# Layer 1's first half: one list of tokens for the experts, or one for each quarter

## The chip, the cores and the metric

The kernel runs on one core of a Trainium2 chip. It is one launch that computes a whole network of four layers. The metric is the device time of that launch in microseconds, as the median of several runs. A core has a matrix engine (TensorE, PE in the profile, with its weight loads as PEld), three engines for elementwise work (VectorE as DVE, ScalarE as ACT, GpSimd as POOL) and SyncE (SP), which here only issues transfers. Every engine runs its own instructions in order and waits on semaphores for the others.

## The reference

Input and output are x of shape (4, 1024, 128) in float32. Each of the four layers does two steps, and after each step x becomes layernorm(x + step(x)):

- Layer 0: a scan over the sequence with a small positional basis ("l0_attn"), then a linear layer whose input and weight are rounded to six-bit values with one scale for 32 of them ("l0_ffn").
- Layer 1: a diagonal complex state-space scan ("l1_attn"), then a mixture of experts.
- Layer 2: causal attention with 16 heads and rotary positions ("l2_attn"), then a mixture of 8 experts with low-rank corrections, 2 per token.
- Layer 3: a Toeplitz mix, then a mixture of 32 experts, 4 per token.

The change is about layer 1's mixture. It has 16 experts of width 128 in four groups. A token takes the two best groups, and in them its four best experts:

```python
scores = sigmoid(x @ router_w.T)          # (tokens, 16)
# two groups by the sum of their two best (scores + bias), then 4 experts
tw = scores[chosen] / sum(scores[chosen]) * 2.5
routed = sum_e tw[e] * (silu(x @ gate_w[e]) * (x @ up_w[e])) @ down_w[e]
out = routed + (silu(x @ sh_gate) * (x @ sh_up)) @ sh_down
```

No step of layer 1 or of layer 0 mixes tokens backwards in time: a token depends on earlier positions of its own row only.

## The kernel before

x stays in on-chip memory as 32 tiles of 128 tokens by 128 values. The sequence is cut into four quarters of 256 positions; with the 4 rows of the batch a quarter is 8 tiles. The same first half (quarters 0 and 1, `self.first`, a `Part` named "a") goes through layer 0 and layer 1's scan, and then its experts run while the second half (quarters 2 and 3) is still in layers 0 and 1.

Layer 1's experts work on a list in device memory. For a part with nt tiles:

- `l1_route` (from L751) computes scores, groups, the mask of the four experts and the weights on DVE; `positions` (L1235) turns the mask into a position in the list for each token and expert (L1276), so that tokens of one expert lie together and every expert begins at a multiple of 128 rows. It also writes the expert of each list tile (`ids`) and the number of list tiles in use (`used`).
- `spread` (L1313) copies token rows to their places: four indirect transfers per tile, issued on POOL (L1301).
- `small_experts` (L1718) walks over the list in groups of four list tiles. `inputs` loads a group (L1332, on SP; the load waits for all the scatters of the list) and transposes it on PE; `up` does the gate and up products on PE, silu on ACT (L1748) and the product with it on DVE (`hg`, L1749); `turn` transposes the result; `down` does the last product, copies it out of PSUM (L1763 on ACT or L1766 on DVE, `yg`) and stores it on SP (L1767). Two groups are loaded ahead.
- A list has room for every possible routing, (nt x 128 x 4 + 127 x 16) rows rounded up to 4 tiles. `small_experts` runs straight-line over the likely length, nt x 4 + 8 tiles rounded up to 4; for what may lie above that, `rest_of` (L1354) puts one `If` on all engines, each of which reads `used` first (L1358, the branch shows as L1359). It then marks the list as made.
- `collect` (L1381) brings results back: four gathers per tile on POOL (L1301, into one buffer `yt` of the pool `yp`, of which there are five) and four adds per tile on DVE (L1392), x += weight x row. The gathers wait for the stores of the list. `l1_close` (L829) collects a quarter at a time, normalizes it (L192 to L209), stores it (`xsave`, L836) and transposes it for layer 2.

The order on each engine is the order in which Python generators are run. `mix` (L238) runs a main generator and, after each of its steps, as many steps of a side generator as the step's estimated microseconds times a pace pay for; instructions of the side are ordered behind those of the main that were already issued. `chain` runs generators one after the other, `abreast` runs several side by side by their estimated times, and `when` (L1819) yields idle steps until a condition holds. The work around the change is, in `all` (L1887 to L1914):

1. `l1_route(a)` after l1_attn of quarters 0 and 1.
2. l0_attn of quarters 2 and 3, with the scatters of list a beside it.
3. The shared experts and the experts of list a as main; beside them l0_ffn and then l1_attn of quarters 2 and 3, at pace 2.0 and without draining what is left.
4. What is left of that side, abreast with `l2_weights` (L1418), as main, with `l1_close(a)` beside it. `l2_weights` builds 24 blocks of layer 2's expert weights: a scaled copy on ACT (L1434), products on PE into a PSUM tile "s", a copy to `we` on ACT (L1444; three buffers), a store on SP (L1446). PSUM has two buffers of the tag "s", which l0_ffn, l1_attn, `turned` and `l2_weights` share in this stage.
5. Layer 2's attention for the first half of the heads' work, `l2_attn(0)` (its first rotation is L928). It begins with normalized quarters 0 and 1.

l0_ffn's rounding (`quantize`) is a chain between DVE and POOL: L483 to L486 on DVE, L489 on POOL, L492 to L496 on DVE, L499 on POOL, L500 on DVE, L501 on POOL, L502 and L503 on DVE. After it POOL adds the bias (L529). l1_attn of a quarter begins with PE products that DVE takes up at L645, scans at L649, turns at L660 to L668, adds at L676 and norms at L209.

Of the kernel before, what the change touches and what calls it, by code (L numbers as in the profile page):

```python
# [40 lines left out]
E1, F1, NG1, TKG1, K1 = 16, 128, 4, 2, 4  # L41
# [15 lines left out]
class Part:  # L57
# [3 lines left out]
    def __init__(self, name, q0, nq, rows=None, lg0=None):  # L61
        self.name, self.q0, self.nq, self.lg0 = name, q0, nq, lg0
        if rows is None:
            self.order = list(range(q0 * QT, (q0 + nq) * QT))
        else:
            self.order = [tile_of(b, 2 * q + k) for b in rows for q in range(q0, q0 + nq) for k in range(2)]
        self.t0, self.nt = q0 * QT, len(self.order)
# [7 lines left out]
class Kernel:  # L75
    def __init__(self, ctx, tc, ins, out, cols, consts, rows):
        self.tc, self.nc, self.ins, self.out = tc, tc.nc, ins, out
        self.count = itertools.count()
        nc = self.nc
        self.const = self.pool(ctx, "const")  # L80
        self.small = self.pool(ctx, "small", 3)
        self.routes = self.pool(ctx, "routes")
        self.side = self.pool(ctx, "side", 2, space=PSUM)
        dram = self.pool(ctx, "dram", space=DRAM)

        self.cols_t = self.load(self.const, ins["cols"])
        self.cst_t = self.load(self.const, ins["consts"])
        self.x = self.tile(self.const, [P, NT, D], "x")
        self.xT = self.tile(self.const, [P, NT * P], "xT")
        nrow = ins["rows"].shape[1]  # L90
        self.rows_t = self.tile(self.const, [P, nrow], "rows")
        nc.gpsimd.dma_start(out=self.rows_t, in_=ins["rows"].to_broadcast([P, nrow]))
        self.col = {k: self.cols_t[:, a:b] for k, (a, b) in cols.items()}
        self.cst = {k: self.cst_t[:, a:b] for k, (a, b) in consts.items()}
        self.row = {k: self.rows_t[:, a:b] for k, (a, b) in rows.items()}
        self.ident = self.cst["ident"]
        self.eps = self.tile(self.const, [P, 1], "eps")
        nc.vector.memset(self.eps, LN_EPS)
        self.halfpi = self.tile(self.const, [P, 1], "halfpi")
        nc.vector.memset(self.halfpi, math.pi / 2)  # L100
        self.ones = self.tile(self.const, [P, E3], "ones")
        nc.vector.memset(self.ones, 1.0)
        self.rnd = self.tile(self.const, [P, 1], "rnd")
        nc.vector.memset(self.rnd, RND)
        self.zero = self.tile(self.const, [P, D], "zero")
        nc.gpsimd.memset(self.zero, 0.0)
        self.flag = self.tile(self.const, [1, 1], "flag", I32)
        self.hm = self.tile(self.const, [P, 4], "hmg")

        self.first, self.rest = Part("a", 0, 2), (Part("b", 2, 1), Part("c", 3, 1))  # L110
        self.parts = (self.first, *self.rest)
        self.by_rows = (
            Part("a", 0, 2, range(B), 0), Part("m", 2, 2, (0, 1), NT // 2), Part("n", 2, 2, (2, 3), 3 * NT // 4)
        )

        self.rows_done = 0

        self.listed = set()

        self.traced, self.latest = nc.cur_bb.bb.instructions, {}  # L120
        self.now = self.moved_by = 0.0
        self.moved = []

        self.lists, self.route = {}, {}
        self.both = (self.first, Part("r", 2, 2))
        for lay, ne, k in (("l1", E1, K1), ("l2", E2, K2), ("l3", E3, K3)):
            for pt in {"l1": self.both, "l2": self.by_rows, "l3": self.parts}[lay]:
                tl = -(-((pt.nt * P * k + (P - 1) * ne) // P) // 4) * 4
                self.lists[lay, pt.name] = (
                    self.tile(dram, [tl * P, D], f"{lay}r{pt.name}"), self.tile(dram, [tl * P, D], f"{lay}y{pt.name}"), tl  # L130
                )
        self.wall2 = self.tile(dram, [P, E2 * 3 * F2], "wall2")
        self.xsave = self.tile(dram, [P, NT, D], "xsave")

        self.ksave = self.tile(dram, [P, B, BLK], "ksave")
        self.vsave = self.tile(dram, [P, B, 4, (NH + 1) * VW], "vsave")
# [1230 lines left out]
    def zero_lists(self, *lays):  # L1367

        for (lay, name), (rows, ys, tl) in self.lists.items():
            if lay not in lays:  # L1370
                continue
            part = next(p for p in (*self.parts, *self.by_rows, *self.both) if p.name == name)
            ne, k = {"l1": (E1, K1), "l2": (E2, K2), "l3": (E3, K3)}[lay]
            for t, at in ((rows, 0), (ys, self.likely(part, ne, k))):
                if at < tl:
                    self.nc.sync.dma_start(
                        out=t[at * P :, :].rearrange("(t p) d -> p t d", p=P),
                        in_=self.zero.unsqueeze(1).to_broadcast([P, tl - at, D]),
                    )
# [507 lines left out]
    def all(self):  # L1887
        a, rest = self.first, self.rest
        b, c = rest
        r = self.both[1]  # L1890
        a2, m2, n2 = self.by_rows
        with ExitStack() as ctx:
            lgp = self.pool(ctx, "l2lg")
            self.l2_lg = self.tile(lgp, [P, NT, E2], "lg")
            with ExitStack() as early:

                self.l0_setup(early)
                self.l2_wr = self.load(lgp, self.ins["l2_wr"])
                self.run(self.l0_attn((0, 1)))
                self.l1_setup()  # L1900
                self.l2_setup()
                self.zero_lists("l1")
                self.run(self.l0_ffn((0, 1)))
                self.run(self.l1_attn((0, 1)))

                self.run(self.l1_route(a))
                self.run(self.mix(self.l0_attn((2, 3)), self.spread("l1", a, K1)))
                self.zero_lists("l2", "l3")
                with ExitStack() as c2:
                    wall = self.l1_wall(c2)  # L1910
                    yp = self.pool(c2, "l1ya", 5, right=True)
                    side = self.chain(self.l0_ffn((2, 3), True), self.l1_attn((2, 3), True))
                    self.run(self.mix(self.chain(self.l1_shared(a), self.l1_experts(a, wall)), side, 2.0, False))
                    self.run(self.mix(self.abreast(self.l2_weights(), side), self.l1_close(a, yp)))  # L1914
            with ExitStack() as c2:
                wall = self.l1_wall(c2)
                self.run(self.mix(self.l2_attn(0), self.chain(self.l1_route(r), self.spread("l1", r, K1))))
                wall2, loads = self.l2_wall(c2, True)
                yp = self.pool(c2, "l1yr", 5, right=True)
                self.run(self.mix(self.chain(self.l1_experts(r, wall), self.l1_shared(r)), self.chain(loads, self.routed(a2))))  # L1920
                self.run(self.mix(self.l2_experts(a2, wall2), self.l1_close(r, yp)))
            listed = lambda name: lambda: name in self.listed
# [6 lines left out]
            with ExitStack() as c3:  # L1929
                with ExitStack() as c2:  # L1930
                    wall = self.l2_wall(c2)
# [7 lines left out]
                yp = self.pool(c3, "l3y", 8)  # L1939
# [25 lines left out]
        with self.tc.If(bad > 0):  # L1965
            with ExitStack() as ctx:
# [9 lines left out]
                for p in self.parts:  # L1976
                    self.run(self.onward(p))
                    with ExitStack() as c2:
                        sw, wall = self.l3_wall(c2)
# [167 lines left out]
```

## Time and profile before

The runs before took 2413.85, 2411.06 and 2410.7 us, a median of 2411.06. The profiled execution took 2413.21 us; its span, from the first to the last instruction on record, is 2411.4 us.

| engine | busy us | share of the span |
|---|---|---|
| PE | 1616.9 | 67% |
| DVE | 1263.6 | 52% |
| ACT | 825.0 | 34% |
| POOL | 722.6 | 30% |

The mean granted TensorE clock is 0.818 of full speed. The stages around the change, by the timeline of the trace:

| stage | from | to |
|---|---|---|
| l1_route(a) on DVE | 245.57 | 275.3 |
| scatters of list a (64) | 268.9 | 381.2 |
| first load of the list; first up-product | 411.93 | 424.87 |
| experts, 18 groups, to the last store | 424.87 | 501.9 |
| gathers (64) | 505.25 | 622.94 |
| last add of the list | 624.65 | 625.0 |
| L928, first rotation of l2_attn(0) | 632.63 | |

How to read the rows that are shown below: a timeline row has start, duration, engine, line, operation, output and inputs by the program's names, and in brackets the engine's idle time before it and what ended it. "issue" and "remote" are idle times that the profile can put down to nothing it records. A row of waits says which engine and line waited for which, how long in total, how many times and the longest. A row of a tile has the shortest, median and longest duration in ns.

### The profile page before, as it was taken

Reading aid. Unit: us, or ns where it says so; the run is one execution under the profiler, and the core shown is the slowest. Engines: PE = TensorE matmul, PEld = TensorE weight load, DVE = VectorE, ACT = ScalarE, POOL = GpSimd, SP = SyncE. Lnnn points to the kernel's source line nnn. Section 1 sums busy time; section 2 is a strip of 40 time slices with the busy share of each in tenths; the row PEclk is TensorE's granted clock in tenths of the full one; section 3 lists DMA queues with packets and bytes.
Section 4 is the critical chain, followed back from the end, with each engine's and each line's share of the span. In section 5 each row is a group of like instructions: output and inputs, shape, how many; then the busy total and the mean of one; then the engine's idle time right before and its main releaser. Section 6 shows DMA issues by size and latency. Waiting matters only on the chain. (4 is left out here: it accounts for less than half of the span.)

```text
span 2411.4 us, 27036 instructions
## 1 busy us (share of the span) xinstructions
PE 1616.9 (67%) x9017; PEld 967.3 (40%) x9017; DVE 1263.6 (52%) x3630; ACT 825.0 (34%) x1180; POOL 722.6 (30%) x681
## 2 busy tenths in 40 slices
PE   7626876975661778487969787887745798357160
PEld 3214333853320337345623232344523486245160
DVE  8957894655570565224545675473611265236233
ACT  6701571422330333122236564642201164223030
POOL 1031484135227000435132002002272200735725
PEclk9856887988785888788979998988977899678575
DMA  9930002334101016212130000031321131222232
GB/s 309 288 112 0 20 34 90 112 115 160 62 31 53 15 34 200 83 44 74 38 106 21 1 1 16 3 114 40 143 85 35 44 112 46 76 79 62 89 89 68
DMA packets 215530, 187.10 MB, mean 78 GB/s; under 512 B 16528, under 2 KB 194064, under 8 KB 214864
## 3 DMA queue, kind: packets, MB, share of 16 engines
q1 hardware_dynamic: 194672, 142.29, 18.7%
q0 software_dynamic: 20704, 42.86, 5.8%
q8 instruction: 84, 1.38, 0.2%
q14 instruction: 70, 0.57, 0.1%
HBM read 88.49 MB, written 96.60 MB: 77 GB/s over the span
## 5 line engine op out<-in xcount | busy, mean ns | idle before, releaser
L1055 ACT ACTIVATE pr<-sc 128x1024 f32<-128x1024 f32 x288 | 279.7, 1021 | 319.9 <-PE sc L157 184.9
L157 PE MATMUL gu<-ld,xgT 128*128 x640 | 177.4, 423 | 88.8 <-issue 38.7
L157 PE MATMUL sc<-qm,kT 32*128 32x512 f32 (+3 forms) x1536 | 199.2, 558 | 13.7 <-issue 12.3
L157 PE MATMUL s<-pr,va 128*32 128x512 f32 (+3 forms) x1536 | 177.1, 528 | 46.0 <-issue 26.2
L157 PEld LDWEIGHTS gu<-ld,xgT 128*128 128x128 f32 x640 | 127.5, 210 | 119.1 <-issue 49.7
L165 PE MATMUL tp<-ld,hg 128*128 128x128 f32 x624 | 104.0, 289 | 92.1 <-ACT hT L167 38.0
L169 DVE COPY hT<-tp 128x512 f32<-128x512 f32 x118 | 81.0, 686 | 159.3 <-remote 73.9
L157 PE MATMUL gu<-wall,xgT 128*128 x304 | 156.1, 640 | 2.7 <-ACT xgT L167 2.0
L1061 DVE TENSOR_TENSOR pr<-pr,ld 128x512 f32<-128x512 f32 (+1 forms) x160 | 92.2, 581 | 100.6 <-ACT pr L1055 98.5
L165 PEld LDWEIGHTS tp<-ld,hg 128*128 128x128 f32 x624 | 81.5, 149 | 144.7 <-issue 46.9
L165 PE MATMUL tp<-ld,xg 128*128 128x128 f32 x396 | 68.9, 305 | 102.1 <-DMA xg<-l3rc 48.5
L1749 DVE TENSOR_TENSOR hg<-sg,gu 128x256 f32<-128x256 f32 x160 | 65.8, 417 | 134.9 <-ACT sg L1748 95.8
L167 ACT COPY xgT<-tp 128x512 f32<-128x512 f32 x99 | 58.0, 586 | 213.0 <-PE tp L165 91.1
L157 PEld LDWEIGHTS sc<-qm,kT 32*128 32x128 f32 x1536 | 84.8, 197 | 113.6 <-issue 77.4
L1507 ACT ACTIVATE sg<-gu 128x512 f32<-128x512 f32 x76 | 45.2, 597 | 225.7 <-PE gu L157 109.4
L1748 ACT ACTIVATE sg<-gu 128x256 f32<-128x256 f32 x160 | 61.1, 385 | 163.2 <-PE gu L157 80.9
L1301 POOL DMA_INDIRECT l1ra<-x,posl1a x64 | 93.1, 1455 | 59.5 <-DVE posl1a L1276 40.3
L157 PEld LDWEIGHTS s<-pr,va 128*32 128x32 f32 x1536 | 38.9, 113 | 156.6 <-issue 109.5
L1509 DVE TENSOR_TENSOR hg<-sg,gu 128x512 f32<-128x512 f32 x76 | 51.7, 682 | 92.1 <-ACT sg L1507 48.7
L1301 POOL DMA_INDIRECT yt<-l1yr,posl1r x64 | 60.9, 951 | 124.1 <-DVE x L1392 79.3
L165 PEld LDWEIGHTS tp<-ld,xg 128*128 128x128 f32 x396 | 52.4, 158 | 107.6 <-issue 59.0
L1301 POOL DMA_INDIRECT l1rr<-x,posl1r x64 | 61.7, 965 | 99.5 <-DVE posl1r L1276 80.3
(440 smaller groups left out, 3498.8 us busy)
## 6 DMA issues: line engine op xcount, KB each, us to landing
wall<-wall SPq DMA_DIRECT2D x16, 768.0 KB
l3ra<-zero SPq DMA_DIRECT2D x1, 6144.0 KB
ld<-in_l_w SPq DMA_DIRECT2D x2, 3072.0 KB
wall<-we SPq DMA_DIRECT2D x24, 256.0 KB
ld<-in_l_w SPq DMA_DIRECT2D x1, 6144.0 KB
l1ra<-zero SPq DMA_DIRECT2D x1, 5120.0 KB
l1rr<-zero SPq DMA_DIRECT2D x1, 5120.0 KB
xg<-l3ra SPq DMA_DIRECT2D x20, 256.0 KB
```

Source lines behind the costliest of these rows:

```text
L157: return self.nc.tensor.matmul(out, lhsT, rhs, start=start, stop=stop)
L165: nc.tensor.transpose(pt[:, k * P : (k + 1) * P], s, self.ident)
L167: nc.scalar.copy(dst, pt[:, : n * P])
L169: nc.vector.tensor_copy(dst, pt[:, : n * P])
L1055: nc.scalar.activation(pr, sc[h], AF.Exp)
L1061: nc.vector.tensor_tensor(d, d, cst["tril"].unsqueeze(1).unsqueeze(1).to_broadcast([P, 2, n, P]), ALU.mult)
L1301: ins = self.nc.gpsimd.indirect_dma_start(**kw)
L1507: nc.scalar.activation(sg, gu[:, 0, :], AF.Silu)
L1509: nc.vector.tensor_tensor(h, sg, gu[:, 1, :], ALU.mult)
L1748: nc.scalar.activation(sg, pg[:, :, 0, :], AF.Silu)
L1749: nc.vector.tensor_tensor(h[:, 2 * c : 2 * c + 2, :], sg, pg[:, :, 1, :], ALU.mult)
```

## The change

The first half gets two lists, "a0" for quarter 0 and "a1" for quarter 1, in place of list "a"; the second half's list "r" stays. Both are routed one after the other at the place where "a" was routed, and their scatters follow each other beside l0_attn. The experts of a0 and then those of a1 run as the main work. The side of that stage gets a second strand beside l0_ffn and l1_attn: when list a0 is made, `l1_close(a0)` begins, with the same five buffers. What is left of both strands goes on in the next stage, whose own side is now only `l1_close(a1)`. By the formulas above a list of 8 tiles has 48 tiles of room and a likely length of 40, ten groups; a list of 16 tiles has 80 and 72, 18 groups.

```diff
+        self.early = (Part("a0", 0, 1), Part("a1", 1, 1))
...
-            for pt in {"l1": self.both, "l2": self.by_rows, "l3": self.parts}[lay]:
+            for pt in {"l1": (*self.early, self.both[1]), "l2": self.by_rows, "l3": self.parts}[lay]:
...
-            part = next(p for p in (*self.parts, *self.by_rows, *self.both) if p.name == name)
+            part = next(p for p in (*self.parts, *self.by_rows, *self.both, *self.early) if p.name == name)
...
-                self.run(self.l1_route(a))
-                self.run(self.mix(self.l0_attn((2, 3)), self.spread("l1", a, K1)))
+                self.run(self.l1_route(a0))
+                self.run(self.l1_route(a1))
+                self.run(self.mix(self.l0_attn((2, 3)), self.chain(self.spread("l1", a0, K1), self.spread("l1", a1, K1))))
                 self.zero_lists("l2", "l3")
                 with ExitStack() as c2:
                     wall = self.l1_wall(c2)
                     yp = self.pool(c2, "l1ya", 5, right=True)
-                    side = self.chain(self.l0_ffn((2, 3), True), self.l1_attn((2, 3), True))
-                    self.run(self.mix(self.chain(self.l1_shared(a), self.l1_experts(a, wall)), side, 2.0, False))
-                    self.run(self.mix(self.abreast(self.l2_weights(), side), self.l1_close(a, yp)))
+                    listed = lambda name: lambda: name in self.listed
+                    side = self.abreast(
+                        self.chain(self.l0_ffn((2, 3), True), self.l1_attn((2, 3), True)),
+                        self.chain(self.when(listed("made l1a0")), self.l1_close(a0, yp)),
+                    )
+                    both = self.chain(self.l1_shared(a), self.l1_experts(a0, wall), self.l1_experts(a1, wall))
+                    self.run(self.mix(both, side, 2.0, False))
+                    self.run(self.mix(self.abreast(self.l2_weights(), side), self.l1_close(a1, yp)))
```

More of the change, by code (lines that the diff above doesn't have):

```diff
@@ L1890, in all @@
         r = self.both[1]
+        a0, a1 = self.early
         a2, m2, n2 = self.by_rows
```

## The prediction

> **What bounds the kernel now.** I read the windows table first, split where the work around layer 1's experts changes hands: experts alone (440 to 470), experts with a quantise chain beside them (470 to 505), then the collecting of the list beside the layer 2 weights and layer 1's attention of quarters 2 and 3 (505 to 625). Columns: stretch, length, busy time and count of PE, weight loads, VectorE (DVE), ScalarE and GpSimd (POOL), TensorE clock, DMA share, GB/s.
>
> ```profile
> 440.00:470.00 30.00, 29.54 (x202) 27.30 (x201) 21.28 (x70) 14.37 (x31) 1.19 (x1) 1.00 0.48 143
> 470.00:505.00 35.00, 26.63 (x181) 23.20 (x180) 26.23 (x61) 10.86 (x23) 8.30 (x4) 0.99 0.31 92
> 505.00:540.00 35.00, 23.38 (x76) 12.42 (x77) 14.88 (x36) 7.84 (x19) 22.39 (x20) 0.77 0.38 130
> 540.00:580.00 40.00, 34.12 (x136) 18.88 (x135) 27.77 (x90) 12.00 (x28) 23.44 (x21) 0.96 0.53 180
> 580.00:625.00 45.00, 11.85 (x41) 6.09 (x39) 20.68 (x96) 7.46 (x13) 23.86 (x24) 0.65 0.35 112
> ```
>
> The experts are bound by PE (29.54 of 30 us). Behind them nothing is full: PE 69.35, DVE 63.33, POOL 69.69 of 120 us. That stage is set by order, so I read what waits in it: the waits from 497 to 640 (total, times, longest), then the gathers on POOL and DVE's timeline.
>
> ```profile
> ACT we L1444 <- issue: 47.7, 11, 12.5
> PE s L165 <- DVE x L209: 36.7, 3, 19.7
> POOL yt L1301 <- DVE x L1392: 29.4, 2, 17.0
> POOL yt L1301 <- DMA l1ya<-yg: 22.0, 1, 22.0
> ```
>
> ```profile
> 505.25 1.01 POOL L1301 DMA_INDIRECT yt<-l1ya,posl1a  x1 [21.98 <-DMA l1ya<-yg]
> 506.56 0.96 POOL L1301 DMA_INDIRECT yt<-l1ya,posl1a  x1 [0.30 <-issue]
> ...
> 550.47 0.95 POOL L1301 DMA_INDIRECT yt<-l1ya,posl1a  x1 [17.03 <-DVE x L1392]
> ...
> 606.26 0.95 POOL L1301 DMA_INDIRECT yt<-l1ya,posl1a  x1 [12.37 <-DVE x L1392]
> ```
>
> ```profile
> 518.69 1.29 DVE L645 TENSOR_TENSOR b<-s,wi 128x512 f32<-128x512 f32 x2 [11.05 <-PE s L157]
> ...
> 548.27 2.19 DVE L1392 SCALAR_TENSOR_TENSOR x<-yt,wkl1a,x 128x128 f32<-128x128 f32 x8
> ```
>
> The 64 gathers start 3.4 us after the last expert work (501.9) and come 1.25 us apart, 80 us in all; they stop twice, because the adds that free the five buffers stand in DVE's order behind quarter 2's attention (548.27) and quarter 3's (602). So two things in series set the stage: layer 1's attention, quarters 2 then 3, and the last gathers. Layer 2's attention takes its first rotation (L928) at 632.63, which is 127.4 us after the first gather. From there both kernels have the same order on every engine, so a shift of L928 should reach the end unchanged.
>
> One stretch is unlike the rest:
>
> ```profile
> 590.08 0.17 DVE L177 TENSOR_SCALAR rstd<-rstd 128x8 int32<-128x8 int32 x1 [1.85 <-remote]
> 590.28 0.43 DVE L908 MEMSET va<- 128x448 f32 x1
> 592.90 0.24 DVE L180 TENSOR_TENSOR nwt<-rstd 128x8 f32<-128x8 f32 x1 [2.18 <-issue]
> ```
>
> From 580 to 598 DVE gets one small instruction per 2 us and PE waits 19.7 us for L209; ScalarE's copies of the weights unit (L1444) have three of their 11 gaps here, up to 12.5 us. It follows the 3 MB load issued at 569.15. In 543 to 546 the same chain runs at 0.2 us an instruction, so this costs about 18 us. The trace does not show what starves it.
>
> **Routing (two lists).** List 1 is quarter 0's, list 2 quarter 1's. A list for each quarter runs the routing code twice. Quarter 0's part can fill DVE's idle 4.28 us before 232.9 and 5.49 us before 245.57. Routing before takes DVE from 245.57 to 275.3, some 30 us, about a third in pieces whose cost hardly shrinks with half the tokens (60 instructions at 0.15 to 0.3 us, 0.7 to 0.8 of their time again: 7 to 9 us), and two more activation-table loads at 1.28 us stand on ScalarE. The z-projections of l0_attn queue on PE behind quarter 0's mask products. l0_attn beside the scatters is DVE-bound (37.71 of 40 us in 300 to 340), so what DVE loses is passed on. Bounds 0 and 9 us; I take **+4**, since the idle stretches hide about half. The scatters start earlier and are not on the path: experts wait for the shared experts' weights, and the first expert load is held by PE until 411.93.
>
> **Two more groups and a middle If.** With 16 tiles the list's likely length is 72 tiles, 18 groups of four; with 8 it is 40, so 10 + 10. SP's expert stores give the pace (and where the quantise chain slows it):
>
> ```profile
> 466.52 0.36 SPq L1767 DMA_DIRECT2D l1ya<-yg  x1
> 468.44 0.36 SPq L1332 DMA_DIRECT2D xg<-l1ra  x1
> 469.95 0.36 SPq L1767 DMA_DIRECT2D l1ya<-yg  x1
> 471.98 0.36 SPq L1332 DMA_DIRECT2D xg<-l1ra  x1
> 478.37 0.36 SPq L1767 DMA_DIRECT2D l1ya<-yg  x1
> ```
>
> A group costs 3.54 us, so two cost 7.1. Its tenth store goes out at 469.95: call that E'. After it every engine meets an If; SP cannot issue list 2's first loads before it, where now they are three groups ahead. Refill: store to next transfer 1.7 us (as at 501.9 to 503.59), load 3.3 (a store of the same 256 KB: from 501.9 to the gather it lets go at 505.25), transposes and copy 3 (L165 x8 takes 1.91 us), so the first up-product is at E'+8; from there to the first store 10.5 us (424.87 to 435.34), then 9 periods: E'+50.4 = 520.4, against 501.9. That is **+18.5**, if nothing holds list 2's experts.
>
> What the branch itself costs: DVE passed the If with 0.19 us (row below) and SP with at most 1.7.
>
> ```profile
> 504.21 0.17 DVE L182 TENSOR_SCALAR nwt<-nwt 128x8 f32<-128x8 f32 x1 [0.19 <-DVEq L1359]
> ```
>
> The Trainium skill ("Runtime: NRT & Kernel Launch", Instruction fetch mechanics) speaks against this part: a taken branch whose target lies outside the two prefetched pages stalls the engine for a fetch from memory. By that rule a further stall of a transfer's length, some 2 us by the 1.7 us row, would fall on the PE or DVE and the total be +2. The If here skips the same two groups as the one measured, so I keep the row: nothing beyond the refill.
>
> **Collecting list 1 beside list 2.** In the built order POOL has, between the two Ifs, 16 gathers (tiles 0 to 3) mixed with the quantise steps L499 and L501, and after the second If four more that need no store of list 2. So 20 of quarter 0's 32 gathers may run beside experts; 12 stay, with quarter 1's 32: 44 gathers or 55 us remain, instead of 80. But DVE's order puts 4 adds of tile 0, L500 (which waits for POOL's L499, behind two gathers of tile 1) and 3 adds of tile 1 ahead of list 2's first hg product, and the rest of the adds between the next ones. The gathers begin at E'+3.4; with 1.25 us each, 2.9 us for L529 ahead and some 3 to land, the seventh add is at about E'+17, where hg was ready at E'+10; the sixteenth is at E'+31 to 33, with four groups' hg done. The other six take 21 us and the tail 5: E'+59 rather than E'+50.4, another **+8.5**. Lower bound 0 (adds always in time). Upper bound by these two rows (min/median/max ns):
>
> ```profile
> L1301 POOL DMA_INDIRECT l1ra<-x,posl1a x64: 957/976/3014, 268.9 to 380.2; - x64
> L1301 POOL DMA_INDIRECT yt<-l1ya,posl1a x64: 943/947/2847, 505.3 to 622.0; - x64
> ```
>
> Scatters beside a busy DVE have a mean of 1.455 us, 0.5 over their quiet value. The skill ("SBUF — State Buffer", the "DVE blocks DMA" trap) says why a GpSimd-issued DMA can suffer: its descriptors can't be written while VectorE holds the shared port in a two-port mode. Row: 20 x 0.5 = 10 us more on POOL, about 8 of it ahead of the adds. Rule at its worst, each gather at the 2.85 maximum: 38 us. Beside experts DVE is 21.28 of 30 us busy, less than beside the scatters; I add nothing and keep +8 for the range.
>
> **After the experts.** Call the first gather of list 2 G (3.4 us after the experts, as now). DVE's order puts 14 adds of quarter 0 before L645 of quarter 2. They need 22 gathers, since the tiles of both quarters alternate: 22 x 1.25 + 3 = G+31, where L645 now starts at G+13.4. PE and the weights unit wait too, as only two "s" buffers serve them. Then quarter 2 takes 29.6 us (518.69 to 548.3), adds and quarter 0's norm 7, quarter 3 29 (48.2 now, less the 18 of starvation, rounded), the last 16 adds, quarter 1's norm and first rotation 13: L928 at **G+110** without starvation, **G+128** with it, against G+127.4. The load stands at the same place between the stores, but other work runs with it, so I take half: **-8**, bounds -17 and +1.
>
> **Sum** on the profiled execution's own 2413.21 us (span 2411.4): +4 +18.5 +8.5 -8 = +23, so 2436; on the median of 2411.06 the same +23 gives 2434, and I put **2433**.
>
> **Rivals.** *Faster:* the two attention chains shrink to their own work. PE 69 and DVE 63 of 120 us show that they are mostly waits; if each goes in 22 instead of 29 us, L928 falls to G+95, a gain of 32, and with hg unheld (+18.5) and routing +2 the kernel ends at -12, 2399. It decides once the gain behind the experts passes 22.5. Against it: L645 is tied to 22 gathers. *Slower still:* starvation recurs in full and the gathers run long: +4 +27 +8 +1 = +40, 2451. *Nothing moved:* list 1's gathers get no cover and start at E anyway, DVE isn't held: +18.5 +4 and the stage at -17: about +5, 2416.
>
> **How the numbers follow.** Chances: my sum (+6 to +36) 0.60; slower still 0.16; within 0.2%, which is about 4.8 us and what a measurement here can tell from no change, 0.07; faster 0.17. Faster 0.17, same 0.07, slower 0.76. The range 2402 to 2452 cuts the further half of the faster and of the slowest case; the likeliest alone has 2417 to 2447.
>
> **What would show it.** Last expert store near 528 to 533; hg L1749 waiting for adds or POOL's quantise steps after the first If; 20 gathers before it; L645 of quarter 2 some 31 us after the first gather of list 2; L928 at about 655. Wrong if experts of list 2 run at 3.54 us from the start, if L645 comes within 15 us, or if the stretch of 2 us per instruction grows.

## The result, and the profile after

The changed kernel takes 2448.03 us (median; 2446.24 to 2457.34), the kernel before 2412.45 us in the same comparison: a ratio of 1.015, with a 95% interval of 1.013 to 1.017. It is slower by 35.6 us, where +22 was forecast; the time lies inside the range given. The profiled execution has a span of 2444.4 us, 33.0 more than before.

The landmarks of the stage, read from the timelines of both traces (us from the start of the span):

| landmark | before | after | shift |
|---|---|---|---|
| load of the shared experts' weights | 376.25 | 400.76 | +24.5 |
| first load of a list | 411.93 | 437.18 | +25.3 |
| end of list 1's ten groups (before: the tenth store) | 470.0 | 484.8 | +14.8 |
| last expert store | 501.9 | 555.7 | +53.8 |
| first gather after the experts | 505.25 | 558.88 | +53.6 |
| L645 of quarter 2, after that gather | +13.4 | +29.1 | |
| first rotation (line L928, now L929) | 632.63 | 663.92 | +31.3 |

Lines of the changed kernel from about 112 on have numbers that are one higher. The windows table of the changed kernel, with the columns of the prediction's table: routing; list 1's experts; list 2's; the stage behind them in two parts.

```profile
245.00:300.00 55.00, 18.07 (x80) 8.94 (x80) 29.96 (x140) 24.21 (x23) 36.01 (x36) 0.62 0.11 42
455.00:486.00 31.00, 28.68 (x200) 26.28 (x198) 21.82 (x70) 13.44 (x28) 0.36 (x1) 1.00 0.38 113
486.00:557.00 71.00, 47.57 (x264) 40.99 (x264) 37.31 (x92) 17.30 (x37) 30.54 (x24) 0.78 0.32 93
557.00:605.00 48.00, 21.61 (x65) 11.88 (x66) 17.59 (x41) 7.36 (x17) 33.78 (x32) 0.68 0.36 112
605.00:625.00 20.00, 18.95 (x74) 10.41 (x74) 17.22 (x81) 8.70 (x18) 5.00 (x6) 1.00 0.40 145
```

List 1's experts are still bound by PE (28.68 of 31 us). List 2's are not: PE has 47.57 of 71 us. And a stage for which 4 us were put down has become slow, the routing: no engine is busy for more than 36 of its 55 us. The same stretch of the kernel before has DVE at 50 of 55 us:

```profile
245.00:300.00 55.00, 43.80 (x169) 19.66 (x170) 50.02 (x159) 32.63 (x35) 25.95 (x18) 0.85 0.05 21
```

DVE's timeline of it in the changed kernel:

```profile
280.22 0.31 DVE L1257 TENSOR_SCALAR ptl<-pinc 128x16 f32<-128x16 f32 x1 [0.99 <-DVE pinc L1254]
282.30 0.17 DVE L1258 TENSOR_SCALAR ptl<-ptl 128x16 f32<-128x16 f32 x1 [1.77 <-remote]
282.39 0.28 DVE L1266 TENSOR_TENSOR pinc<-pinc,ptot 128x128 f32<-128x128 f32 x1
283.70 0.17 DVE L1259 TENSOR_SCALAR ptl<-ptl 128x16 f32<-128x16 f32 x1 [1.04 <-DVE pinc L1266]
285.80 0.19 DVE L1261 TENSOR_TENSOR_SCAN pend<-ones,ptl 128x16 f32<-128x16 f32 x1 [1.92 <-remote]
```

This looks like the starved stretch of 580 to 598, in another place: instructions of 0.2 us, 1 to 2 us apart, from 269 to 293, in the routing of quarter 1. What POOL does at that moment, from its timeline:

```profile
287.18 0.96 POOL L1302 DMA_INDIRECT l1ra<-x,posl1a  x1 [0.30 <-issue]
288.44 0.95 POOL L1302 DMA_INDIRECT l1ra<-x,posl1a  x1 [0.30 <-issue]
295.06 1.08 POOL L1302 DMA_INDIRECT l1ra<-x,posl1a  x1 [5.67 <-DVE peq L1295]
```

It issues list 1's 32 scatters without a pause, from 248 to 289.4. DVE is back at its usual pace at 293, 3.5 us after the last of them. In the kernel before, the gathers of that burst ended at 593.9 and DVE was free at 597.8.

Behind the middle If, DVE's timeline shows the order that the prediction described:

```profile
497.33 0.35 DVE L1393 SCALAR_TENSOR_TENSOR x<-yt,wkl1a,x 128x128 f32<-128x128 f32 x1 [0.86 <-DMA yt<-l1ya,posl1a]
500.57 1.23 DVE L501 SCALAR_TENSOR_TENSOR qt<-qt,qt 128x1024 f32<-128x1024 f32 x1 [2.89 <-POOL qt L500]
501.71 0.73 DVE L1393 SCALAR_TENSOR_TENSOR x<-yt,wkl1a,x 128x128 f32<-128x128 f32 x2
504.32 0.35 DVE L1393 SCALAR_TENSOR_TENSOR x<-yt,wkl1a,x 128x128 f32<-128x128 f32 x1 [1.88 <-DMA yt<-l1ya,posl1a]
504.59 0.41 DVE L1750 TENSOR_TENSOR hg<-sg,gu 128x256 f32<-128x256 f32 x1
508.80 1.23 DVE L503 TENSOR_TENSOR qt<-qt,qt 128x1024 f32<-128x1024 f32 x1 [3.80 <-POOL qt L502]
509.94 0.41 DVE L1750 TENSOR_TENSOR hg<-sg,gu 128x256 f32<-128x256 f32 x1
```

Seven adds and L501 stand before list 2's first hg, whose silu was ready at 494.22 (493.84 + 0.38); L503 holds the second. The waits of that window (485 to 557) show who pays, and one wait that no program order explains:

```profile
PE gu L158 <- DVE hg L1750: 12.4, 2, 10.4
ACT sg L1749 <- remote: 7.4, 1, 7.4
DVE qt L503 <- POOL qt L502: 3.8, 1, 3.8
```

In the stage behind the experts, the order is as forecast too; DVE's timeline:

```profile
587.99 2.48 DVE L646 TENSOR_TENSOR b<-s,wi 128x512 f32<-128x512 f32 x4
...
621.63 2.48 DVE L646 TENSOR_TENSOR b<-s,wi 128x512 f32<-128x512 f32 x4 [0.80 <-issue]
...
646.13 2.13 DVE L210 TENSOR_SCALAR x<-x,mv,rstd 128x128 f32<-128x128 f32 x8
```

Quarter 3 goes from L646 to the end of L210 in 26.6 us, where it took 48.2 before: here the starved stretch is gone.

### The profile page after: what moved, and what is told of

Its sections match the earlier page's. It is cut to its first block, busy times and chain, and to the rows that moved or that the text cites. A ratio compares the mean times of both kernels' runs of the same rounds, so it can differ in the third digit from the quotient of the medians.

```text
span 2444.4 us, 27296 instructions
## 1 busy us (share of the span) xinstructions
PE 1614.2 (66%) x9070; PEld 970.2 (40%) x9070; DVE 1277.2 (52%) x3705; ACT 830.9 (34%) x1191; POOL 710.9 (29%) x681
## 5 line engine op out<-in xcount | busy, mean ns | idle before, releaser
L158 PE MATMUL gu<-ld,xgT 128*128 x656 | 186.2, 431 | 107.9 <-issue 36.9
L158 PE MATMUL sc<-qm,kT 32*128 32x512 f32 (+3 forms) x1536 | 198.3, 558 | 16.5 <-issue 14.0
L158 PEld LDWEIGHTS gu<-ld,xgT 128*128 128x128 f32 x656 | 133.9, 216 | 138.7 <-ACT xgT L168 43.0
L1302 POOL DMA_INDIRECT l1ra<-x,posl1a x64 | 80.0, 1250 | 47.3 <-DVE peq L1295 28.4
L158 PE MATMUL yp<-ld,hT 128*128 x656 | 89.9, 279 | 2.1 <-DVE hT L170 1.1
```

Of the source, the lines that this page charges most:

```text
L158: return self.nc.tensor.matmul(out, lhsT, rhs, start=start, stop=stop)
L1302: ins = self.nc.gpsimd.indirect_dma_start(**kw)
```

## The experiments

Three things were to be told apart: what routing twice costs by itself; what the If, the refill and the hold by gathers cost; and whether the starved stretch follows POOL's rows of indirect transfers. The sets of runs fell on different chips, so a kernel is set against the kernel before on its own chip, and against another kernel only where both were there.

| kernel | before there | kernel | ratio (95%) |
|---|---|---|---|
| swap | 2409.23 | 2430.34 | 1.0085 (1.0054 to 1.0115) |
| apart | 2409.23 | 2458.64 | 1.0179 (1.0144 to 1.0214) |
| b_yp9 | 2409.23 | 2413.59 | 1.0023 (0.9995 to 1.0051) |
| swap_late | 2051.57 | 2082.09 | 1.0156 (1.0122 to 1.0190) |
| swap_drain | 2051.57 | 2074.48 | 1.0101 (1.0065 to 1.0136) |
| b_drain | 2051.57 | 2064.76 | 1.0058 (1.0042 to 1.0074) |
| b_yp9_drain | 2051.57 | 2056.77 | 1.0026 (1.0013 to 1.0039) |
| before2 | 2409.70 | 2410.08 | 1.0003 (0.9986 to 1.0020) |
| after2 | 2409.70 | 2449.05 | 1.0155 (1.0110 to 1.0201) |
| swap2 | 2409.70 | 2426.34 | 1.0071 (1.0050 to 1.0092) |
| b_yp9_2 | 2409.70 | 2417.41 | 1.0023 (1.0004 to 1.0042) |
| b_yp9_drain2 | 2406.48 | 2404.27 | 0.9984 (0.9967 to 1.0000) |

**swap: no scatters beside the second routing.** The diff shows the changed argument alone.

```diff
-    self.chain(self.spread("l1", a0, K1), self.spread("l1", a1, K1))
+    self.chain(self.spread("l1", a1, K1), self.spread("l1", a0, K1))
```

> The changed kernel with the two scatter strands in the other order: list 2's scatters first, so that POOL issues nothing before list 2's positions are done. Theory A: the stretch 269 to 292 us, in which DVE gets one dependent instruction per 1 to 2 us, comes from POOL's unbroken row of scatters beside the routing; without it l0_attn's first scan step (302.9) comes 15 to 20 us earlier, the shared experts' loads go from 400 to about 383 us, and the time from 2448 to 2428 to 2434. Rival B: two routings cost these 20 us by their own instructions; then the stretch or its sum stays and the time is within 4 us of 2448.

The same instructions; only, POOL's first scatter now waits for the second routing. The first scatter starts at 278.41, the shared experts' load at 384.25 instead of 400.76, and the time is 2430.34. DVE's timeline in the routing of quarter 1:

```profile
273.63 0.17 DVE L1258 TENSOR_SCALAR ptl<-ptl 128x16 f32<-128x16 f32 x1
273.92 0.17 DVE L1259 TENSOR_SCALAR ptl<-ptl 128x16 f32<-128x16 f32 x1
274.12 0.19 DVE L1261 TENSOR_TENSOR_SCAN pend<-ones,ptl 128x16 f32<-128x16 f32 x1
```

From L1258 to L1261 it now takes 0.5 us, against 3.5 in the changed kernel. Theory A holds: of the +24.5 us, 16.5 (400.76, which apart has on this chip too, less 384.25) are the row of scatters beside the routing, and 8.0 (384.25 less the 376.27 of b_yp9 on the same chip, whose routing is the old one) are the second routing itself. Repeated on another chip as swap2, beside the changed kernel (after2):

> Scatters of list 2 first. Theory A: on a chip without the stall the order of the scatters matters for nothing: the time is within 5 us of the changed kernel's on that chip; on one with it, 12 to 20 us below. Rival B: list 2's scatters first are better by themselves (less beside the routing): 8 us or more below the changed kernel on any chip.

2426.34 against 2449.05 us, 22.7 less, a little more than expected. Rival B, that this order is better on any chip, is not excluded: on the chip without the stall the changed kernel was not run.

**apart: list 1 collected in the next stage.**

```diff
-                    side = self.abreast(
-                        self.chain(self.l0_ffn((2, 3), True), self.l1_attn((2, 3), True)),
-                        self.chain(self.when(listed("made l1a0")), self.l1_close(a0, yp)),
-                    )
+                    side = self.chain(self.l0_ffn((2, 3), True), self.l1_attn((2, 3), True))
...
-                    self.run(self.mix(self.abreast(self.l2_weights(), side), self.l1_close(a1, yp)))
+                    self.run(self.mix(self.abreast(self.l2_weights(), side), self.chain(self.l1_close(a0, yp), self.l1_close(a1, yp))))
```

> The changed kernel with list 1 collected after the experts, ahead of list 2, in the place where the kernel before collects; two lists, two routings and the middle If stay. Theory A: of the 71 us from list 1's last store (485) to list 2's (556), about 20 are the wait of list 2's experts for gathers, adds and the rounding chain; they shrink to 48 to 54. Behind them 64 gathers instead of 44 remain, so the first rotation comes 110 to 128 us after the first gather instead of 105: time 2434 to 2450. Rival B: the 71 us are the price of the If and of a second list; then they stay above 65 and the time is 2453 or more.

The numbers are those of rival B: 75.1 us from list 2's first load to the first transfer of the next stage (486.50 to 561.60; in the changed kernel 70.8, 486.51 to 557.33), and 2458.64. But the run did not take away what it was meant to. POOL has nothing else to do after the If, so it ran list 1's first 20 gathers beside list 2 all the same, now as one row. POOL's timeline, then DVE's:

```profile
499.78 1.99 POOL L1302 DMA_INDIRECT yt<-l1ya,posl1a  x1 [0.15 <-issue]
...
524.75 0.95 POOL L1302 DMA_INDIRECT yt<-l1ya,posl1a  x1 [0.30 <-issue]
601.22 0.94 POOL L1302 DMA_INDIRECT yt<-l1ya,posl1a  x1 [75.52 <-DVE x L1393]
```

```profile
524.14 0.69 DVE L1767 COPY yg<-yp 128x512 f32<-128x512 f32 x1 [13.59 <-remote]
```

The hold by adds is gone, and in its place DVE stands for 13.59 us for a product that PE had finished at 510.6. It decides nothing on the If, and says that a row of gathers can cost list 2 as much as DVE's order does. Then the 44 other gathers start at 601.22 only, since the five buffers come free behind quarter 2's attention.

**swap_late: really no gather beside list 2.** The diff is against apart, the changed arguments alone.

```diff
-    self.chain(self.spread("l1", a0, K1), self.spread("l1", a1, K1))
+    self.chain(self.spread("l1", a1, K1), self.spread("l1", a0, K1))
...
-    self.chain(self.l1_close(a0, yp), self.l1_close(a1, yp))
+    self.chain(self.l1_close(a1, yp), self.l1_close(a0, yp))
```

> Scatters of list 2 first, as in the run with the order swapped, and no gather beside the experts: the close of list 2 comes first, after the experts, then that of list 1, so that POOL's gathers wait for list 2's stores. Theory A: gathers beside list 2's experts are what stretches list 1's last store to list 2's last store to 71 to 75 us, by holding DVE's order and by a stall of the other engines in an unbroken row of gathers; without them it is 48 to 54 us. 64 gathers follow, with the first rotation 110 to 130 us after the first of them: time 2420 to 2440. Rival B: the If, the refill and two more groups cost the 71 us by themselves: they stay above 65 and the time is 2440 to 2455.

The first gather comes at 528.07. By the same count list 2 takes 56.8 us (469.62 to 526.45): some 3 us above theory A's window, and far below 65. The first rotation is at 636.5, 108.4 us after the first gather. So the If, the refill, ten groups and the rounding chain of quarter 3 make up 57 us on this chip, where the changed kernel has 71 on its own. Here too the first hg is held, by the rounding chain alone. ScalarE's silu, then DVE:

```profile
476.99 0.38 ACT L1749 ACTIVATE sg<-gu 128x256 f32<-128x256 f32 x1 [1.36 <-PE gu L158]
```

```profile
483.04 1.23 DVE L503 TENSOR_TENSOR qt<-qt,qt 128x1024 f32<-128x1024 f32 x1 [2.45 <-POOL qt L502]
484.18 0.41 DVE L1750 TENSOR_TENSOR hg<-sg,gu 128x256 f32<-128x256 f32 x1
```

The silu was ready at 477.37, and hg starts 6.8 us later. This chip runs the kernel before in 2051.57 us; the absolute times expected were those of the other chips. By the ratio, 1.0156, the time is rival B's, though list 2's length is not.

**swap_drain: gathers beside list 2, with stops.** The diff is in `collect`, on top of swap.

```diff
+            if lay == "l1" and part.name[0] == "a" and t % 3 == 2:
+                look = nc.gpsimd.tensor_copy(self.tile(self.small, [P, 1], "dr"), yt[:, k - 1, :1])
+                self.moved.append(look.ins.name)
             late.append((t, yt, self.moved_by + 4.0))
```

> Scatters of list 2 first, and after the gathers of every third tile a one-column copy on POOL that reads the last of them, so that POOL stops until it has landed (3 to 4 us) and a row of gathers is never longer than 12 without a stop. Theory A: an unbroken row of indirect transfers stalls the other engines' handshakes until it ends; the stall of 5 to 7 us beside list 2's experts goes, and list 1's last store to list 2's takes 60 to 66 us; time 3 to 10 us below the swapped kernel's 2430. Rival B: the stalls have another cause; then the stops add 10 to 15 us of gathering and the time is the same or up to 10 us longer.

On the same chip as swap_late: 64.1 us for list 2 (472.69 to 536.80), 7.3 more than without gathers. From list 2's end to the first rotation (635.18) it takes 98 us, against 110 in swap_late. So collecting beside list 2 costs some 7 us there and gives back more than that behind. The median is 7.6 us below swap_late's, but the two intervals overlap; both kernels stay 1.0 to 1.6% slower than the kernel before. Whether the stops took away a stall can't be said here, since this chip shows none (below).

**b_yp9, b_drain, b_yp9_drain: the kernel before, with nine gather buffers, with the stops, and with both.**

```diff
-                    yp = self.pool(c2, "l1ya", 5, right=True)
+                    yp = self.pool(c2, "l1ya", 9, right=True)
```

> The kernel before with nine gather buffers instead of five. Theory A: the two stops of the gathers (17.0 and 12.4 us) are waits for buffers only; the 64 gathers run through and end near 590 instead of 623, the first rotation then waits for quarter 3's norm and comes 10 to 18 us earlier: time 2394 to 2402. Rival B: a longer unbroken row of gathers slows DVE's small instructions more than it saves; the stretch of one instruction per 2 us grows and the time is within 4 us of 2412 or above it.

Wrong: 1.0023. The first row of gathers grew from 20 to 36, and with it a stall. POOL's timeline and DVE's, in b_yp9:

```profile
552.38 0.94 POOL L1301 DMA_INDIRECT yt<-l1ya,posl1a  x1 [0.30 <-issue]
585.19 0.94 POOL L1301 DMA_INDIRECT yt<-l1ya,posl1a  x1 [31.86 <-DVE x L1392]
```

```profile
538.60 0.30 DVE L193 BATCH_NORM_AGGREGATE mv<-bn 128x2 f32<-128x6 f32 x2
556.78 0.69 DVE L676 TENSOR_TENSOR x<-s,x 128x512 f32<-128x512 f32 x1 [17.88 <-remote]
```

L676 waits for a product that PE had done at 539.75, and gets it at 556.78, 3.5 us after the row ended (553.3). No instruction of the starved stretch of the kernel before is slow any more: it is not these instructions, and not the 3 MB load, which comes at 585.17 here. On another chip b_yp9_2 gives 1.0023 again.

> The kernel before with nine gather buffers. Theory A: on a chip without the stall the gathers run through, the last add is done near 590 and quarter 3's norm near 585 sets the rest; the first rotation comes at 598 to 606, 5 to 12 us before the kernel before's there, and the time falls by as much. Rival B: the order of DVE's adds, not the buffers, sets the end; the time is within 4 us of the kernel before's.

> The kernel before with the same stop after every third tile's gathers. Theory A: the stretch of one instruction per 2 us (580 to 598) goes and quarter 3's norm is done near 584 instead of 602; five stops put some 15 us on the gathers, which with their five buffers end near 620 again, so the first rotation comes 0 to 6 us earlier: time 2404 to 2412. Rival B: the stretch stays at the same instructions (it belongs to DVE's program or to the 3 MB load) and the time rises to 2415 to 2428.

> The kernel before with nine buffers and the stops. Theory A: neither the wait for buffers nor the stall is left; the 64 gathers take 80 + 15 us, to about 602, and the first rotation comes near 615 instead of 633: time 2390 to 2400. Rival B: with nine buffers and no stops the stall of 17.9 us was in the same place of the program whatever POOL does; it stays and the time is 2408 to 2420.

Both ran on the chip of swap_late. With the stops the first rotation is at 624.17 (b_drain) and 611.88 (b_yp9_drain), yet the times are 1.0058 and 1.0026: taken as ratios, the numbers of the rivals. Theory A's numbers were worked out from a trace with the stall, and this chip has none to take away. What is left is probably the price of the stops; that is not shown, since no trace of the kernel before was kept from this chip.

**before2 and after2: the two kernels once more.**

> The kernel before, unchanged, for a profile beside the three others on one chip. On a chip that shows the stall behind rows of indirect transfers: first rotation near 633 and 570 to 598 as in the first profile. On a chip without it: first rotation 608 to 614, quarter 3's norm done near 583, no row of DVE in which dependent instructions are 1 to 3 us apart.

> The changed kernel, unchanged. Theory A (the stall took some 20 us of the routing and 7 us beside list 2's experts, but also 18 us of the kernel before, behind its experts): on a chip without it the shared experts' loads come 5 to 9 us later than in the kernel before, not 24, list 1's last store to list 2's takes 62 to 66 us instead of 71, the first rotation comes 96 to 105 us after the first gather of list 2, and the time is 15 to 28 us above the kernel before's. Rival B: the routing costs its 24 us anywhere; then the difference is 35 us or more.

A chip with the stall: first rotation at 633.69 and 663.14, shared experts' load at 376.81 and 398.76, 70.4 us for list 2, 1.0155. The first comparison is reproduced. The difference of 39 us is in rival B's range (35 or more), but swap2 on the same chip, with its load at 382.60, puts 16.2 of the load's 22.0 us down to the order of the scatters. Theory A's case of a chip without the stall was not measured for the changed kernel.

**b_yp9_drain2: the last one again, on a chip with the stall.**

> The kernel before with nine buffers and a stop after every third tile's gathers, once more, to see it on a chip that shows the stall. Theory A: no row is longer than 12 gathers, so the stall (17.9 us with nine buffers and no stops, 18 us in the kernel before) does not begin; the first rotation comes near 612 to 616 instead of 633, and the time is 12 to 22 us below the kernel before's on the same chip. Rival B: the stall comes from the count of transfers in flight or from their total, not from the unbroken row; it stays, and the time is within 5 us of the kernel before's or above. On a chip without the stall: 1.00 to 1.005 of the kernel before, as measured.

0.9984 (0.9967 to 1.0000): nearer to nothing than to the 12 to 22 us expected. The gathers of one row of twelve (538.00 to 552.7) and the stop after it on POOL, then DVE:

```profile
551.79 0.94 POOL L1301 DMA_INDIRECT yt<-l1ya,posl1a  x1 [0.30 <-issue]
554.41 0.18 POOL L1406 COPY dr<-yt 128x1 f32<-128x1 f32 x1 [1.67 <-DMA yt<-l1ya,posl1a]
```

```profile
541.42 2.17 DVE L209 TENSOR_SCALAR x<-x,mv,rstd 128x128 f32<-128x128 f32 x8
555.12 1.29 DVE L645 TENSOR_TENSOR b<-s,wi 128x512 f32<-128x512 f32 x2 [11.53 <-remote]
```

ScalarE stands from 544.6 to 550.2, when the row is six gathers old, so PE has the products that L645 waits for at 552.5 only, and DVE goes on 2.4 us after the row. A row of twelve is no safe length. No version here beats the kernel before by more than its interval.

## Why the prediction came out as it did

*Direction and range were right. The middle term of the sum was met by two errors that offset each other; the outer two were off by 20.5 and 14.3 us in opposite directions, both where the starved stretch comes in. That the sum came within 14 us of the measured 35.6 is luck.*

- **Routing, +4 (0 to 9): measured +24.5.** This is the step that failed, in the sentence "The scatters start earlier and are not on the path". They were counted as work of POOL's own, and it was not asked what they do to the engine beside them. The instructions' own cost is 8.0 us (swap) and 7.7 (swap_late's load at 383.38 against b_drain's 375.66, on one chip), near the upper bound; 16.5 us are DVE slowed beside the row of scatters, shown by the swap.
- **Experts, +18.5 +8.5 = +27: measured +29.1** (53.6 - 24.5, by the first gather behind them). List 1 ends 9.7 us earlier against its start than the tenth group did before (+14.8 against +24.5), which the sum did not have. From the first load of the list to the first store it takes 18.1 us instead of 23.4 (PE's 91 products there take 14.09 us at a granted clock of 1.00, before 18.05 at 0.78); from there to the tenth store 29.5 instead of 34.6, with 199 products instead of 235, since at a list's end no products of further groups stand between. List 2 takes 71 us where 59 was worked out. The mis-sized term is the way from list 1's last store to list 2's first, 18.5 us in the working: 26.6 without gathers (swap_late), of which the rounding chain's hold is 6.8, and 37.9 in the changed kernel, where the first hg is held for 10.4. The nine groups behind it, 31.9 us in the working (at 3.54 a group, which is the pitch of two loads; the first ten stores before lie 3.85 apart), take 30.1 and 33.0. By one chip's runs collecting beside list 2 costs 7.3 us, with swap_drain's stops in it (8.5 was forecast). The changed kernel's other 7 are near the 7.4 us that ScalarE waits with no visible cause while POOL's ten gathers of 509 to 522 run; that these are the same stall was not isolated.
- **Behind the experts, -8 (between -17 and +1): measured -22.3** (105.04 against 127.38 us from gather to rotation). L645 came at G+29.1 (G+31 forecast), the two quarters took 33.6 and 26.6 us (36.6 and 29). The case "without starvation", G+110, was the right one, and half of each was taken. Why the stretch did not recur is not shown. Quarter 2's norms fall between POOL's rows (the first stops at 602, the next begins at 618); quarter 3's, starved before, fall from 634 to 648, where the second row, of only twelve, ends at 637.
- **The rivals.** "Slower still" had the right total (2451) by a wrong road: it had the starvation recur behind the experts, and it came up in the routing. L645 tied to 22 gathers, the argument against the faster rival, held. "Nothing moved" did not happen: 20 gathers run before the second list's stores.
- **The rules weighed.** On the branch, keeping to the row was right as far as runs can tell: at the middle If each engine's branch takes 0.05 to 0.25 us, and SP's next load leaves 1.7 us after list 1's last store, as worked out. On gathers held up beside a busy DVE, the rule looked at the wrong victim: the 20 gathers stay near 0.95 us (two reach 1.9), and it is the other engines that stand.

In sum: +24.5 +29.1 -22.3 = +31.3 at the first rotation, +33.0 over the span, +35.6 by the medians.

## What to carry to other kernels

Work moved to an idle queue has to be costed by what it does to its new neighbours, not only by what it takes on its own engine: here, on the chips that show the stall, 32 scatters that nobody waited for cost their neighbour 16 us. A stretch in which several engines run one instruction at a time for no visible reason should be traced to what runs without a pause beside it before a change is priced, because the stretch moves with that. And splitting a pipelined stage costs a refill (and whatever order puts into it) that has to be earned back in full behind it.

## What the runs showed of the hardware

On the chips of the first comparison and of three of the four later sets of runs, a row of indirect transfers on POOL, one each 1.25 us, comes in many places with PE, ScalarE and DVE standing or getting one instruction per 1 to 2.8 us, until 2.4 to 3.9 us after the row's end (b_yp9_drain2, the kernel before). The largest case is not in this change at all: beside the 64 scatters of list r in layer 2's attention. PE's timeline of the kernel before, then its windows table:

```profile
759.72 0.37 PE L157 MATMUL s<-pr,va 128*32 128x128 f32 x1 [2.43 <-issue]
762.51 0.37 PE L157 MATMUL s<-pr,va 128*32 128x128 f32 x1 [2.43 <-issue]
765.32 0.37 PE L157 MATMUL s<-pr,va 128*32 128x128 f32 x1 [2.43 <-issue]
```

```profile
700.00:800.00 100.00, 26.95 (x134) 10.66 (x134) 20.37 (x77) 9.27 (x10) 61.74 (x64) 0.56 0.11 42
```

and the windows table of b_drain, which has the same work there, on the chip where the kernel before takes 2051.57 us:

```profile
700.00:800.00 100.00, 83.93 (x764) 41.39 (x764) 69.12 (x192) 46.54 (x48) 60.66 (x59) 0.93 0.15 57
```

PE has 83.93 us of work instead of 26.95 beside nearly the same count of scatters. So the stall belongs to some chips and not to all. How much of the difference between them it is can be read from one kernel on both: b_yp9_drain, and b_yp9_drain2 with the stall, have the same 1180 ScalarE instructions in the same order. The last one starts 356 us later with the stall. Of this, some 340 us gather in those 980 us in which, for the most part, a row of indirect transfers runs or has ended less than 3.5 us before, and some 17 in the other 1416.

Not every row stalls. List a's 64 scatters (268 to 380.5 in these two traces, one each 1.75 us beside a DVE that is busy for 106 of 125 us) do not move the two apart: the gap between them stays at 0.95 to 1.05 us. And the changed kernel's 32 gathers from 558.88 to 602 end beside a DVE at its usual pace (588 to 598).

What the stall is stays open. It hits instructions for which the profile shows nothing to wait for (PE's products above), so the supply of instructions comes to mind: the Trainium skill ("Runtime: NRT & Kernel Launch", Instruction fetch mechanics) says that each engine's sequencer fetches its pages by a DMA queue of its own. But in the 100 us of the kernel before shown above, the queues for instructions moved one packet, in 1.11 us, so pages that arrive late do not explain one product per 2.8 us. No run tells it from late semaphores, or from an effect of the recording itself.
